# Ending a four-layer graph kernel: one chain of factors for all 26 tiles instead of two, halves in the last row block, a second slot for the last sums

## The chip, the cores and the metric

The kernel runs on one core of one Trainium2 chip. Times are microseconds of device time for one execution. The time before is the median of three runs. The profile is one more execution, taken by the hardware profiler; its span runs from the first to the last instruction of the core, and its own time is a little longer than its span.

## The reference, cut to what matters

Four graph layers follow each other on a node matrix of 3327 x 64 (padded to 26 tiles of 128 nodes) with a dense 0/1 adjacency matrix. Each is a pre-norm residual layer: `h = relu(layernorm(x))`, `x = x + layer(h, adj)`. The change concerns the fourth layer alone, a hyperbolic attention:

```python
left, right = x_t @ w_att[:D, 0], x_t @ w_att[D:, 0]
adj_att = sigmoid(left[:, None] + right[None, :] + b_att[0]) * adj
x_local = logmap(x[:, None, :], x[None, :, :], c)          # for every pair of nodes
support_t = einsum('ij,ijd->id', adj_att, x_local)         # sums over neighbours
return proj(expmap(x, support_t, c), c)                    # pointwise per node
```

The kernel does not form `x_local`. The logarithm of a pair becomes a weight (an arctangent of a Gram product, plus a constant), so that the sums over neighbours are matrix products of the weights with rows of x. What is left after these sums (`expmap`, `proj` and the residual) is pointwise per node: it comes down to two numbers for each node, here called ah and am, and to `X += Xr*ah + M*am`, where Xr holds the layer's scaled input and M the sums.

## The kernel before, in words

The function `hyperbolic_series` serves the first and the fourth layer; the fourth call (`then is None`, with r, `done` and `checks`) is the one that changes. Its nodes i are cut into four chunks of 4, 3, 3 and 3 tiles in each of two halves (`chunks`, line 380): half o holds tiles 0 to 12 or 13 to 25, and one chunk covers columns of both halves at once, so that a work tile is 128 x 2 x 512 or 128 x 2 x 384. For every chunk a loop goes over the 26 row blocks b of the neighbours. That is K = 104 work tiles, listed in `tiles`.

The order on ACT, DVE, PE and POOL in the loop is written out by hand (`tc.manual_schedule`, closed by `region.close()` on line 945). For work tile k:

- `sigmoid(k)` (line 610): ACT makes the sigmoid (L614), POOL multiplies it with the adjacency mask, which is fp8 in this call (L616);
- `products(k)` (line 618): PE makes the Gram product in a PSUM slot (L627, L628), one of four;
- `angle(k)` (line 630): ACT takes the arctangent in place (L633);
- `weights(k)` (line 635): DVE adds a constant and multiplies with the masked sigmoid (L637);
- `sums(k)` (line 640): PE adds the tile to the chunk's sums. L646 uses every tile by itself, one product for each half o; L654 takes the tiles in pairs, after the second one.

After row block 25 of a chunk, the closures in `later` run: `out_of` copies the two parts of the sums from PSUM to SBUF (ACT, L664), `back` turns both parts with six PE transposes into one slot (L673), and `to_m` and `to_m2` form, for that chunk's columns, the inner product hm with Xr (L684, L692), M0 (L685), the norm mm (squares L686 on ACT, sum L693) and M itself (L690).

`factors` (line 701) is a generator of some 55 small DVE operations on one column of numbers per tile, with one tanh on ACT (L780). It holds two inverse roots by bit tricks (`root_by_bits`, L128 to L142), and most of its steps use the result of the step before. Before the change it runs twice: for `early` = the first ten tiles of each half (20 tiles), and for `late_` = the last chunk (6 tiles). The first 16 steps of the early one stand in the loop's iteration j = K/2 (line 919). Then `both` issues late and early steps in turn, and when early has its factors, `moves` for these 20 tiles stands between the remaining late steps: 20 scalings of M on ACT (L877, one tile each), and on DVE four times Xr*ah (L870), four times X+Xr (L882) and four times X+M (L886). `done` stores these tiles (L2073, SP queue). Moves and a store for the late six tiles follow.

At the very end every engine loads a flag from SBUF and branches on it (L2124; a fallback that isn't taken on these data stands behind the branch). SP does this after it has issued the last store.

Of the kernel before, what the change touches and what calls it, by code (L numbers as in the profile page):

```python
# [14 lines left out]
AF = mybir.ActivationFunctionType  # L15
OP = mybir.AluOpType
# [33 lines left out]
def tile_gnn4(ctx: ExitStack, tc: tile.TileContext, x, adjT, att0, b0, w1, bias1, w_gat, a_gat,  # L50
# [8 lines left out]
    def room(**kw):  # L59

        return tc.tile_pool(reuse_waits="tile", **kw)
# [288 lines left out]
    def hyperbolic_series(r, params, ok, masks=None, done=None, ahead=None, then=None, checks=None):  # L350
# [18 lines left out]
        with ExitStack() as st:  # L369
# [232 lines left out]
            def by_tiles(t, c):  # L602

                return (t.rearrange("p (o t) d -> p o t d", o=2) if len(t.shape) == 3 else
                        t.rearrange("p (o t) -> p o t", o=2))[:, :, c[0]:c[0] + c[1]]

            def new(name, c, dtype=F32, rows=P, **kw):
                return wk.tile([rows, 2, W], dtype, name=name, **kw)[:, :, :c[1] * P]

            def sigmoid(k):  # L610

                c, b = tiles[k]
                sig = sigs[k] = new("sig", c, bufs=7)
                A.activation(sig, leftB[c], AF.Sigmoid, bias=right[:, b:b + 1])  # L614
                adj = adjs.pop(k) if masks is None else halves(masks[b // 2][:, b % 2, :], c)
                G.tensor_tensor(sig, adj, sig, op=OP.mult)  # L616

            def products(to):

# [14 lines left out]

            def weights(k):
                slot, sig = Ls.pop(k), sigs[k]
                V.scalar_tensor_tensor(sig, slot[:, :, :tiles[k][0][1] * P], PC, sig, op0=OP.add, op1=OP.mult)  # L637
                slots.append(slot)

            def sums(k):  # L640
# [25 lines left out]
                    slots.append(acc.pop(c))  # L666

            def back(j, c, a):
                slot = slots.pop(0)
                for o in range(2):  # L670
                    for i in range(c[1]):
                        cs = slice(i * P, (i + 1) * P)
                        PE.transpose(slot[:, o, cs], a[:, o, cs], ident)  # L673
                later[j, 1] = lambda: to_m(j, c, slot)

            def to_m(j, c, slot):
                pm = slot[:, 0, :c[1] * P].rearrange("p (t o d) -> p o t d", o=2, d=D)
                if ahead is not None and c == chunks[-1]:
                    prod = ahead.same.rearrange("p o i -> p (o i)").bitcast(F32)[:, :4 * c[1] * D].rearrange(
                        "p (k o t d) -> p k o t d", k=2, o=2, d=D)  # L680
                else:
                    prod = wk.tile([P, 2, 2, 4, D], F32, name="prod", bufs=1)[:, :, :, :c[1], :]
                pm0 = slot[:, 1, :c[1] * P].rearrange("p (t i o d) -> p o t i d", i=2, o=2, d=32)
                V.tensor_mul(prod[:, 0], by_tiles(Xr, c), pm)  # L684
                V.reduce_sum(by_tiles(M0, c), pm0[:, :, :, :, 0], axis=AX.X)  # L685
                A.activation(prod[:, 1], pm, AF.Square)  # L686
                later[j + 1, 0] = lambda: to_m2(j + 1, c, slot, pm, prod)
# [164 lines left out]
                both = value_of(factors(lambda name: tp.tile([P, T], F32, name=name), (0, HT)))  # L852
                return [f.rearrange("p o t -> p (o t)") for f in both]

            def place_in_loop(name):

                return checks.adjs[2][:, len(places) * T:(len(places) + 1) * T]

            found = {}

            def of_tiles(c):
                found[c] = yield from factors(place_in_loop, c)

            def moves(c, pieces):


                ah, am = found[c]

                def scaled(a, f, ts):
                    V.tensor_mul(a, a, f[:, :, :, None].to_broadcast([P, f.shape[1], f.shape[2], D]))  # L870

                cut = [(slice(o, o + n), slice(t, t + m)) for o, n, t, m in pieces]
                for os, ts in cut:
                    for o in range(os.start, os.stop):
                        for t in range(ts.start, ts.stop):
                            m = by_tiles(M, c)[:, o, t, :]
                            A.activation(m, m, AF.Copy, scale=am[:, o, t:t + 1])  # L877
                for os, ts in cut:
                    x, a = by_tiles(X, c)[:, os, ts], by_tiles(Xr, c)[:, os, ts]
                    scaled(a, ah[:, os, ts], ts)  # L880
                    yield
                    V.tensor_add(x, x, a)  # L882
                    yield
                for os, ts in cut:
                    x, m = by_tiles(X, c)[:, os, ts], by_tiles(M, c)[:, os, ts]
                    V.tensor_add(x, x, m)  # L886
                    yield
                done(c)

            def both(one, two):  # L890

                for _ in one:
                    next(two, None)

            early, late_ = (0, 10), chunks[-1]
            moving = of_tiles(early) if done is not None else iter(())

            sigmoid(0)
            for j in range(-1, K // 2 + (5 if then is None else 1)):
                for k in (2 * j - 2, 2 * j - 1):  # L900
                    if 0 <= k < K:
                        sums(k)
                for i in range(2):
                    k = 2 * j + i
                    products(2 * j + 3 + i)
                    if 0 <= k < K:
                        weights(k)
                    if i == 0 and (j, 0) in later:
                        later.pop((j, 0))()
                    products(2 * j + 4)  # L910
                    if k + 2 < K:
                        angle(k + 2)
                    if k + 3 < K:
                        if masks is None and k + 5 < K:
                            load(k + 5)
                        sigmoid(k + 3)
                    if i == 1 and (j, 1) in later:
                        later.pop((j, 1))()
                    if j == K // 2:
                        for _ in range(8):  # L920
                            next(moving, None)
                if at(2 * j + 10, 1):
                    columns(at(2 * j + 10, 1))
                if ahead is not None:
                    ahead.step(j)
                if checks is not None:
                    checks.step(j)
                if then is not None and j == K // 2 - 1:
                    table_of(AF.Exp)

            if then is not None:
                then(SimpleNamespace(Xr=Xr, M=M, slots=slots, later=later, factors=all_factors, close=lp.close,
                                     ahead=ahead, close_all=hs.close))
                return
            def of_early():
                yield from moving
                yield from moves(early, [(o, 1, t, 5) for o in range(2) for t in (0, 5)])

            rest = of_early()
            both(of_tiles(late_), rest)  # L940
            for _ in rest:
                pass
            for _ in moves(late_, [(0, 1, 0, 3), (1, 1, 0, 3)]):
                pass
            region.close()
            lp.close()

    def hyperbolic(att, b_att, r, min_norm, min_norm2):

# [1115 lines left out]
        for ts in HALVES:  # L2065
            nc.sync.dma_start(X[:, ts, :], x.rearrange("p (t d) -> p t d", d=D)[:, ts, :])

    def store():
        nc.sync.dma_start(out.rearrange("p (t d) -> p t d", d=D), X)

    def store_tiles(c):
        ts = slice(c[0], c[0] + c[1])
        nc.sync.dma_start(out.rearrange("p (h t d) -> p h t d", h=2, d=D)[:, :, ts, :], X2[:, :, ts, :])  # L2073

    ok = const.tile([P, 4], F32, name="ok")
    load()
# [9 lines left out]
    with ExitStack() as ms:  # L2086
        mid, rs = [ms.enter_context(ExitStack()) for _ in range(2)]
        masks = [None] * (T // 2)
        degs = []

        def make_masks(ks):
            pool = ms.enter_context(room(name=f"masks{ks[0]}", bufs=1, side="right"))
            for k in ks:
                masks[k] = pool.tile([P, 2, NP], F8, name=f"mask{k}")

        def right():
            make_masks(range(T // 2 - EARLY // 2))
            pool = rs.enter_context(room(name="middle", bufs=1, side="right"))
            degs.append(pool.tile([P, NP // 2], F32, name="deg"))
            return degs[0]  # L2100

        make_masks(range(T // 2 - EARLY // 2, T // 2))
        pool = mid.enter_context(room(name="own", bufs=1))
        own = [pool.tile([P, 2, CW], F32, name=f"own{k}") for k in range(2)]
        hyperbolic_series(None, params, ok[:, 0:1], ahead=Ahead(masks, zo, own),
                          then=lambda e: plain_decay(
                              e, right, masks, zo, wt, bias, gru, of_r[0],
                              lambda *a: plain_gat(masks, zo, degs[0], first, wg, gru, *a)))
        rs.close()
        mid.close()  # L2110
        hyperbolic_series(r3, params3, ok[:, 2:3], masks, store_tiles, checks=Late(zo))
    V.reduce_sum(ok[:, 1:2], zo, axis=AX.X)


# [55 lines left out]
```

## Time and profile before

| what | us |
|---|---|
| median of the three runs | 728.15 (726.80 to 729.39) |
| the profiled execution's own time | 726.02 |
| its span | 724.3 |
| PE busy | 628.6 (87%) |
| DVE busy | 543.4 (75%) |
| ACT busy | 539.4 (74%) |
| POOL busy | 430.3 (59%) |
| last PE work of the loop (start of the last L654 group) | 696.30 |
| DVE's last addition to X starts / the last store is issued | 716.9 / 717.3 |

A group's line in the profile names line, engine and operation, then `out<-in` with the shapes, a count, busy time and the mean of one in ns, then the idle time before it and what ended it. In the timeline the first two columns are start and duration in us from the span's start. POOL's spans are rough, and the ends of matmuls are modelled.

### The profile page before, as it was taken

The page shows a single profiled execution, that of the slowest core. Times are in us where ns is not written, and L with a number is a line of the kernel's source. Part 1 is how long each engine was busy: PE and PEld are TensorE (multiplying, and loading weights), DVE is VectorE, ACT ScalarE, POOL GpSimd, SP SyncE. Part 2 cuts the span into 40 slices and gives each one's busy share as a digit, 9 for nine tenths or more (in the row PEclk, how much of TensorE's full clock was granted, in tenths as well). Part 3 has the DMA queues.
Part 4 walks back from the last instruction along what each step waited for, and adds up shares of the span by engine and source line. Part 5 has one row for each costly group of instructions (what it writes and reads, how often), then busy time and mean ns, then how long its engine had stood idle before and what let it go on. Part 6 is the DMA issues. An engine that isn't in the chain of part 4 may idle for free.

```text
span 724.3 us, 12042 instructions
## 1 busy us (share of the span) xinstructions
PE 628.6 (87%) x4227; PEld 253.2 (35%) x4227; DVE 543.4 (75%) x1055; ACT 539.4 (74%) x705; POOL 430.3 (59%) x326
## 2 busy tenths in 40 slices
PE   0799999989999799989998997169999999999950
PEld 0522233333333243435445642052223333333310
DVE  6867778777777799999746239887667878777776
ACT  2788888888888785687871586258888889888833
POOL 2699999989999301116620000048888787888820
PEclk9999999999999999999999999569999999999985
DMA  3898898888888716489940000203334334444001
GB/s 64 307 296 268 265 277 264 276 274 271 271 251 279 262 44 243 133 289 349 403 183 2 1 1 1 94 19 94 95 95 134 106 116 149 119 119 118 2 4 50
DMA packets 61751, 119.26 MB, mean 165 GB/s; under 512 B 9552, under 2 KB 34032, under 8 KB 61680
## 3 DMA queue, kind: packets, MB, share of 16 engines
q1 hardware_dynamic: 57328, 118.38, 50.7%
q10 hardware_dynamic: 4352, 0.02, 0.3%
q8 instruction: 35, 0.57, 0.3%
q14 instruction: 36, 0.29, 0.1%
HBM read 115.64 MB, written 0.88 MB: 161 GB/s over the span
## 4 chain that ended last, share of the span: by engine, by line
PE 64%; DVE 16%; POOL 5%; issue 4%; DMA 4%; ACT 3%; SPq 2%; ACTq 1%; POOLq 0%; DVEq 0%
PE slot L646 18%; PE slot L654 10%; PE slot L627 9%; PE slot L628 8%; PE slot L1580 6%; PE slot L1879 5%; POOL sig L616 5%; PE slot L1594 4%; DMA adj<-in 3%; DVE same L1475 2%; PE slot L1995 1%; ACT sig L614 1%; DVE mask L1563 1%; DVE sig L637 1%; DVE X L1633 1%
## 5 line engine op out<-in xcount | busy, mean ns | idle before, releaser
L637 DVE SCALAR_TENSOR_TENSOR sig<-slot,sig 128x768 f32<-128x768 f32 (+1 forms) x208 | 212.6, 1022 | 110.6 <-POOL sig L616 109.4
L633 ACT ACTIVATE slot<-slot 128x768 f32<-128x768 f32 (+1 forms) x208 | 177.3, 852 | 56.7 <-PE slot L628 56.5
L616 POOL TENSOR_TENSOR sig<-adj,sig 128x768 f32<-128x768 f32 (+1 forms) x104 | 201.1, 1963 | 14.8 <-ACT sig L614 10.5
L614 ACT ACTIVATE sig<-leftB,right 128x768 f32<-128x768 f32 (+1 forms) x208 | 203.3, 977 | 0.1
L616 POOL TENSOR_TENSOR sig<-mask,sig 128x768 f32<-128x768 fp8e4 (+1 forms) x104 | 173.3, 1679 | 39.9 <-ACT sig L614 39.0
L646 PE MATMUL slot<-sig,Xr 128*64 128x384 f32 (+1 forms) x832 | 169.6, 526 | 7.5 <-DVE sig L637 7.4
L627 PE MATMUL slot<-XC,XT 128*128 128x384 f16 (+1 forms) x416 | 142.2, 342 | 2.7 <-ACT sum L664 1.7
L628 PE MATMUL slot<-XF,XE 73*128 73x384 f16 (+1 forms) x416 | 141.3, 340 | 0.0
L654 PE MATMUL slot<-sig,X 128*32 128x384 f32 (+1 forms) x832 | 94.2, 525 | 0.0
L1586 ACT ACTIVATE w<-slot,ebias 128x832 bf16<-128x832 f32 x76 | 69.2, 952 | 25.1 <-PE slot L1580 24.7
L646 PEld LDWEIGHTS slot<-sig,Xr 128*64 128x64 f32 x832 | 49.6, 135 | 89.1 <-issue 61.0
L627 PEld LDWEIGHTS <-XT 128*128 128x128 f16 x416 | 40.6, 98 | 93.8 <-issue 67.4
L1580 PE MATMUL slot<-mask,rest 128*128 128x416 fp8e4 x208 | 53.9, 341 | 5.2 <-ACT adj L1586 2.8
L1580 PE MATMUL slot<-mask,after 128*128 128x416 fp8e4 x208 | 53.3, 339 | 1.1 <-DVE deg L1604 1.1
L628 PEld LDWEIGHTS <-XE 73*128 73x128 f16 x416 | 40.8, 98 | 28.5 <-issue 4.2
L1475 DVE TENSOR_SCALAR_CACHE_REDUCE same<-late 128x832 fp8e4<-128x832 f32 x48 | 48.4, 1009 | 0.0
L219 POOL TENSOR_TENSOR mask<-mask,offdiag 128x128 fp8e4<-128x128 fp8e4 x26 | 15.8, 617 | 46.7 <-PE slot L1580 46.7
L436 POOL MEMSET X<- 128x832 f32 x2 | 1.6, 792 | 67.8 <-DVE o L2024 67.8
L1879 PE MATMUL slot<-mask,own 128*64 128x416 fp8e4 x416 | 38.8, 340 | 2.2 <-DVE deg L1604 2.2
L654 PEld LDWEIGHTS slot<-sig,X 128*32 128x32 f32 x832 | 16.4, 108 | 67.7 <-issue 66.1
L1594 PE MATMUL slot<-w,h 128*64 128x416 bf16 x304 | 34.0, 345 | 0.0
L542 PE MATMUL pt<-ident_h,Xp 128*64 128x128 f16 x32 | 2.6, 313 | 35.5 <-ACT Xp L481 35.5
(351 smaller groups left out, 686.1 us busy)
## 6 DMA issues: line engine op xcount, KB each, us to landing
adj<-in SPq DMA_DIRECT2D x78, 384.0 KB, 4.6
late<-in SPq DMA_DIRECT2D x48, 416.0 KB, 3.2
adj<-in SPq DMA_DIRECT2D x17, 832.0 KB, 7.2
adj<-in SPq DMA_DIRECT2D x27, 512.0 KB, 5.1
ahead<-in SPq DMA_DIRECT2D x14, 832.0 KB, 8.2
ahead<-in SPq DMA_DIRECT2D x16, 416.0 KB, 5.9
own<-in SPq DMA_DIRECT2D x16, 416.0 KB, 5.7
own<-in SPq DMA_DIRECT2D x8, 832.0 KB, 6.6
```

Source lines behind the costliest of these rows:

```text
L614: A.activation(sig, leftB[c], AF.Sigmoid, bias=right[:, b:b + 1])
L616: G.tensor_tensor(sig, adj, sig, op=OP.mult)
L627: PE.matmul(L[:, o, :c[1] * P], XT[:, rows], XC[c][:, o, :], start=True, stop=False)
L628: PE.matmul(L[:, o, :c[1] * P], XE[:KE, rows], XF[c][:, o, :], start=False, stop=True)
L633: A.activation(L, L, AF.Arctan, scale=PA / SX ** 2)
L637: V.scalar_tensor_tensor(sig, slot[:, :, :tiles[k][0][1] * P], PC, sig, op0=OP.add, op1=OP.mult)
L646: PE.matmul(acc[c][o * D:(o + 1) * D, 0, :n], Xr[:, b, :], sigs[k][:, o, :], start=b == 0, stop=b == T - 1)
L654: PE.matmul(acc[c][q:q + 32, 1, :n], X0[:, b - 1 + i, :], w[:, o, :], start=b == 1, stop=b == T - 1, tile_position=(0, q))
L1580: PE.matmul(cnt[o][:, h, :BK], w, cols(k, o, h), start=w is after and steps[k][1] == T - 1, stop=True, skip_group_check=True)
L1586: A.activation(ws[k][:, o, :, :], cnt[o][:, :, :BK], AF.Exp, scale=-LN2, bias=ebias)
L1594: PE.matmul(acc[c][o * D:(o + 1) * D, h, :BK], parts[i][:, b, :], w[:, o, h, :], start=b == T - 1 and i == 0, stop=b == 0 and i == 1)
L1879: PE.matmul(acc[k][o * D:(o + 1) * D, :], w, mask[:, o * HP + k * BK:o * HP + (k + 1) * BK], start=n == 0 and i == 0, stop=n == T - 1 and ...
```

## The change

In the fourth layer only:

- Row block 25 of the last chunk (k = 103) goes through POOL (L616) and DVE (L637) as two halves of 128 x 384 instead of one 128 x 768 operation. PE's L646 products of the two halves o wait for their own half.
- Each of the last chunk's two turned parts gets a slot of its own; `to_m` reads the first part from one and the second from the other.
- `factors` runs once for all 26 tiles, after the loop. It stands outside the hand-written order, so that its place in the queues is the scheduler's. The in-loop early steps, `of_tiles`, `moves`, `both` and `place_in_loop` go away; the factors' tiles come from a pool that is opened after the loop's is closed.
- The moves are made on halves of 13 tiles (832 elements a partition): Xr*ah twice, X+Xr twice. M*am is done by ACT for tiles 0 to 21 and by one DVE operation for tiles 22 to 25. Then three additions X+M follow, of 13, 7 and 6 tiles, each with a store of its own: three stores of contiguous tiles with 128 rows instead of two stores of two pieces per partition.

```diff
+            def parts_of(k):
+                return (slice(0, 1), slice(1, 2)) if k == K - 1 and then is None else (slice(0, 2),)
...
-                G.tensor_tensor(sig, adj, sig, op=OP.mult)
+                for os in parts_of(k):
+                    G.tensor_tensor(sig[:, os], adj[:, os], sig[:, os], op=OP.mult)
...
-                V.scalar_tensor_tensor(sig, slot[:, :, :tiles[k][0][1] * P], PC, sig, op0=OP.add, op1=OP.mult)
+                for os in parts_of(k):
+                    V.scalar_tensor_tensor(sig[:, os], slot[:, os, :tiles[k][0][1] * P], PC, sig[:, os],
+                                           op0=OP.add, op1=OP.mult)
...
-                slot = slots.pop(0)
+                to = [slots.pop(0)]
+                to.append(slots.pop(0) if j > K // 2 and then is None else to[0])
...
-                        PE.transpose(slot[:, o, cs], a[:, o, cs], ident)
+                        PE.transpose(to[o][:, o, cs], a[:, o, cs], ident)
...
-                pm0 = slot[:, 1, :c[1] * P].rearrange("p (t i o d) -> p o t i d", i=2, o=2, d=32)
+                pm0 = to[1][:, 1, :c[1] * P].rearrange("p (t i o d) -> p o t i d", i=2, o=2, d=32)
...
-                    if j == K // 2:
-                        for _ in range(8):
-                            next(moving, None)
...
-            rest = of_early()
-            both(of_tiles(late_), rest)
-            for _ in rest:
-                pass
-            for _ in moves(late_, [(0, 1, 0, 3), (1, 1, 0, 3)]):
-                pass
             region.close()
             lp.close()
+            with room(name="hse", bufs=1) as tp:
+                ah, am = all_factors(tp)
...
+                own = slice(T - 4, T)
+                for t in range(own.start):
+                    A.activation(M[:, t, :], M[:, t, :], AF.Copy, scale=am[:, t:t + 1])
+                for ts in HALVES:
+                    scaled(Xr, ah, ts)
+                    added(Xr, ts)
+                scaled(M, am, own)
+                for ts in HALVES[0], slice(T // 2, T - 6), slice(T - 6, T):
+                    added(M, ts)
+                    done(ts)
...
-        nc.sync.dma_start(out.rearrange("p (h t d) -> p h t d", h=2, d=D)[:, :, ts, :], X2[:, :, ts, :])
+    def store(ts=slice(0, T)):
+        nc.sync.dma_start(out.rearrange("p (t d) -> p t d", d=D)[:, ts, :], X[:, ts, :])
```

`scaled(a, f, ts)` multiplies `a[:, ts, :]` in place by the factor of each tile, and `added(a, ts)` adds `a[:, ts, :]` to X in place.

More of the change, by code (lines that the diff above doesn't have):

```diff
@@ L672, in back, with to_m @@
                         cs = slice(i * P, (i + 1) * P)
-                        PE.transpose(slot[:, o, cs], a[:, o, cs], ident)
-                later[j, 1] = lambda: to_m(j, c, slot)
-            def to_m(j, c, slot):
+                        PE.transpose(to[o][:, o, cs], a[:, o, cs], ident)
+                later[j, 1] = lambda: to_m(j, c, to)
+            def to_m(j, c, to):
+                slot = to[0]
                 pm = slot[:, 0, :c[1] * P].rearrange("p (t o d) -> p o t d", o=2, d=D)
@@ L853, in all_factors @@
                 return [f.rearrange("p o t -> p (o t)") for f in both]
[L855 to L896, printed above, removed]
             sigmoid(0)
@@ L934, in hyperbolic_series, with scaled, added @@
                 return
-            def of_early():
-                yield from moving
-                yield from moves(early, [(o, 1, t, 5) for o in range(2) for t in (0, 5)])
-            rest = of_early()
-            both(of_tiles(late_), rest)
-            for _ in rest:
-                pass
-            for _ in moves(late_, [(0, 1, 0, 3), (1, 1, 0, 3)]):
-                pass
             region.close()
             lp.close()
+            with room(name="hse", bufs=1) as tp:
+                ah, am = all_factors(tp)
+                def scaled(a, f, ts):
+                    V.tensor_mul(a[:, ts, :], a[:, ts, :], wide(f[:, ts]))
+                def added(a, ts):
+                    V.tensor_add(X[:, ts, :], X[:, ts, :], a[:, ts, :])
+                own = slice(T - 4, T)
[8 more added lines that the diff above has]
+                    done(ts)
     def hyperbolic(att, b_att, r, min_norm, min_norm2):
@@ L2066, in load @@
             nc.sync.dma_start(X[:, ts, :], x.rearrange("p (t d) -> p t d", d=D)[:, ts, :])
[L2068 to L2072, printed above, removed]
-        nc.sync.dma_start(out.rearrange("p (h t d) -> p h t d", h=2, d=D)[:, :, ts, :], X2[:, :, ts, :])
+    def store(ts=slice(0, T)):
+        nc.sync.dma_start(out.rearrange("p (t d) -> p t d", d=D)[:, ts, :], X[:, ts, :])
     ok = const.tile([P, 4], F32, name="ok")
@@ L2110, in tile_gnn4 @@
         mid.close()
-        hyperbolic_series(r3, params3, ok[:, 2:3], masks, store_tiles, checks=Late(zo))
+        hyperbolic_series(r3, params3, ok[:, 2:3], masks, store, checks=Late(zo))
     V.reduce_sum(ok[:, 1:2], zo, axis=AX.X)
```

## The prediction

> **What bounds the kernel now.** I read the page first (PE is busy 87% of the span), then the timeline of the last 35 us, where the whole change lies. The loop bodies of the fourth layer stay as they are, so PE's bound there stays too. From row block 103 on, one thing waits for the next:
>
> ```profile
> 692.90 1.56 POOL L616 TENSOR_TENSOR sig<-mask,sig 128x768 f32<-128x768 fp8e4 x1 [0.53 <-ACT sig L614]
> 694.50 0.96 DVE L637 SCALAR_TENSOR_TENSOR sig<-slot,sig 128x768 f32<-128x768 f32 x1 [1.14 <-POOL sig L616]
> 695.51 0.87 PE L646 MATMUL slot<-sig,Xr 128*64 128x384 f32 x4 [0.68 <-DVE sig L637]
> 696.30 0.85 PE L654 MATMUL slot<-sig,X 128*32 128x384 f32 x8
> 697.22 0.87 ACT L664 ACTIVATE sum<-slot 128x384 f32<-128x384 f32 x2 [3.70 <-PE slot L654]
> 697.77 0.93 PE L673 MATMUL slot<-ident,sum 128*128 128x128 f32 x6 [0.61 <-ACT sum L664]
> 698.74 0.56 DVE L684 TENSOR_TENSOR prod<-Xr,slot 128x384 f32<-128x384 f32 x1 [0.57 <-PE slot L673]
> 699.46 0.49 ACT L686 ACTIVATE prod<-slot 128x384 f32<-128x384 f32 x1 [1.37 <-DVE M L685]
> 699.99 0.55 DVE L693 TENSOR_REDUCE mm<-prod 128x6 f32<-128x384 f32 x1
> 700.46 0.15 DVE L716 TENSOR_TENSOR late<-M,kb 128x6 f32<-128x6 f32 x1
> ```
>
> No engine is full here; it is a relay. At 700.46 the late factors start. The windows show what follows: DVE is busy without a gap until the last addition ends, then 7 us run without any compute.
>
> ```profile
> 700.46:708.72 8.26, 0.00 (x0) 0.00 (x0) 8.09 (x84) 0.43 (x2) 0.00 (x0) 0.50 0.02 6
> 708.72:717.25 8.53, 0.00 (x0) 0.00 (x0) 8.36 (x34) 6.42 (x26) 0.00 (x0) 0.50 0.14 56
> 717.25:724.30 7.05, 0.00 (x0) 0.00 (x0) 0.00 (x0) 0.00 (x0) 0.00 (x0) 0.50 0.18 61
> ```
>
> Columns: stretch, us, then busy time and count of PE, weight loads, DVE, ACT, POOL. So the late factors take from 700.46 to 715.23 (14.8 us for 6 tiles), since steps and moves of the early tiles stand between them.
>
> The price of a step is in DVE's timeline of the early chain, where it runs alone:
>
> ```profile
> 697.12 0.18 DVE L130 TENSOR_TENSOR late<-late 128x20 f32<-128x20 f32 x1
> 697.34 0.18 DVE L132 TENSOR_TENSOR late<-late 128x20 f32<-128x20 f32 x1
> 697.55 0.18 DVE L134 SCALAR_TENSOR_TENSOR late<-late 128x20 f32<-128x20 f32 x1
> ...
> 715.18 0.36 DVE L870 TENSOR_TENSOR Xr<-Xr,late 128x192 f32<-128x192 f32 x1
> 715.58 0.36 DVE L882 TENSOR_TENSOR X<-X,Xr 128x192 f32<-128x192 f32 x1
> 715.85 0.35 DVE L870 TENSOR_TENSOR Xr<-Xr,late 128x192 f32<-128x192 f32 x1
> 716.24 0.36 DVE L882 TENSOR_TENSOR X<-X,Xr 128x192 f32<-128x192 f32 x1
> 716.51 0.74 DVE L886 TENSOR_TENSOR X<-X,M 128x192 f32<-128x192 f32 x2
> ```
>
> Start to start is 0.21: 0.18 of duration and 0.035 until a dependent step starts. An independent one starts about 0.08 before its forerunner's end (695.37, then 695.46), so 0.10 apart. A 6-wide step takes 0.16, so width costs about 1 ns an element.
>
> [...] the trace's 128x832 multiplication (L480) takes 1024; for 320 [...] L882 takes 491. [...] the square (L686) starts after DVE's L685, which reads the same slot, though it needs nothing of it. [...] L877 takes 332, and 20 of them 4.88 us, 0.244 apart. [...]
>
> **The parts.**
>
> *Halves of block 103.* POOL's two shapes take 1564 ns for 768 and 2025 for 1024 elements (means of L616 by shape): 1.80 ns an element and 0.18 fixed, so a half is 0.87. DVE's L637 takes 0.955 and 1.226: a half is 0.55. POOL ends its halves at 693.77 and 694.64, DVE's second half runs from 694.68 to 695.23 instead of ending at 695.46. PE then has only the second half's products left (the first half's lie beside DVE's second): L646 begins at 695.28, and L654 follows after 0.79-0.36=0.43, at 695.71 instead of 696.30. **Gain 0.6.** Bounds: if a POOL half cost 1.0, DVE would end at 695.5 and PE alone would give 0.35; if it cost exactly half, 0.78, the gain is 0.75.
>
> *Two slots.* DVE's product L684 needs three of the six transposes, 0.46 earlier (0.93/2). M0 (L685) waits for the other three, at about the time L684 ends, so it stalls little. The square waits for L684 alone, no longer for L685: 0.56 earlier (0.46 and 0.10). It releases mm (L693), and mm the chain. **Gain 0.55** (0.4 to 0.6). The second slot is free by then, and nothing is queued behind.
>
> *One chain.* From its queue order I walk the 26-wide chain with 0.182 a step, 0.218 for a dependent one, 0.24 with a pointer operand (as L775 shows), 0.3 for the reciprocal:
> - the first ten operations, up to the third product: 0.99;
> - eleven dependent steps through the first root: 10 x 0.218 + 0.28 = 2.46;
> - to ACT's tanh and back: 0.48, as at 700.99 to 701.44, then 0.21;
> - 24 mixed steps, most independent of their neighbour: 2.53;
> - ten dependent steps through the second root: 2.18, and 0.22 for the last two.
>
> That is 9.07 from the first step to the first move. The early chain's steps in the loop were hidden beside PE's last sums; now all tiles start after them, but the width is nearly free. Bounds: 0.21 to 0.23 a dependent step moves this by 0.25 either way.
>
> *Moves.* DVE: four operations of 832 at 0.94 apart, 3.74; the 256-wide scaling of M, 0.34; three additions of 832, 448 and 384. ACT's 22 scalings start with am: the 13th is done 3.3 after it (earlier than DVE needs it, at 4.1), the 20th 5.0 after. So the second addition waits some 0.1 for ACT. The last one ends 6.2 after the chain. ACT is next in line here: at 0.33 apart it would be late.
>
> So chain and moves take 9.07+6.23=15.3, where 700.46 to 717.25 is 16.8 now. **Gain 1.5** (1.1 to 1.9). In-place X, the pool opened later and the removed in-loop steps I cost at nothing: the queue order shows no new wait of the first steps on another engine, and the in-loop steps stood where DVE waits for PE.
>
> *Stores.* A store is now 128 rows; the trace's 128x832 loads on SP are issued in 0.33, where the last store of 256 pieces takes 0.575. SP loads the flag after it. **Gain 0.24.** The additions end 0.55 or more apart, so three issues at 0.38 don't queue. SP then branches and is away for 2.9 us, before it looks at the stores' semaphores:
>
> ```profile
> SPq L2124 <- SPq L2124: 2.9, 1, 2.9
> ```
>
> Under this the data are hidden: they start 1.3 after the first issue (714.75 to 716.05 now); 852 KB at the 353 GB/s of today's first store (655 KB in packets from 716.05 to 717.91) take 2.4, landing 0.6 (the second's last packet ends at 719.44, its semaphore is up at 720.04). That is 4.3 after the first issue; SP looks at 1.1 (the third issue) + 4.35 = 5.5.
>
> **Sum:** 0.6+0.55+1.5+0.24 = 2.9. Against the profiled execution's own 726.0 us (span 724.3) this gives 723.1, 0.40% less. The median of the runs, 728.15, stands 2.1 above that execution; I take the same 2.9 from it: **725.2 us**.
>
> **Rivals.** *ACT sets the end:* if its scalings go 0.33 apart because they no longer overlap beside 832-wide DVE work, the 22nd is done 7.3 after am, the last addition ends 1.7 later than I have it, and 1.2 is left: 727.0. Against it: 20 of them went at 0.244 beside DVE. *Halves and slots don't show:* if PE's clock sags or the scheduler's waits hold the transposes together, 0.6 and 0.55 are lost: 726.4. Against it: the program's waits are finer already. *More than I count:* the mixed steps pack tighter and POOL's halves are 0.78: 724.1. *Slower, by the stores:* nearly all 852 KB leave in the last 1.1 us, where before 655 KB had left 2.6 us earlier. If 128 rows drain slowly, landing outlasts SP's 2.9 us. From 239 GB/s down (852 KB in 5.5-1.3-0.6=3.6) it costs; at 131 the gain is gone; at 90 (9.5 us, 5.9 over the cover) it is 731.1. Today's second store, of 768 B pieces, moved 197 KB in 0.88, 223 GB/s, so some cost is possible, but 90 needs less than half of that.
>
> **How the numbers follow.** My forecast has 0.58 (its own range 724.4 to 725.9), ACT as bound 0.18, halves and slots without effect 0.14, more than counted 0.05, slower by the stores 0.05. The measurement tells apart about 0.3%, 2.2 us. Faster: 0.58+0.05=0.63; same: 0.32; slower: 0.05. From 723.6 to 727.2 only the stores' case and the edges of the two end cases are left out.
>
> **What would show it.** In the new profile: two POOL halves of some 0.87 and L646 in two pieces; the square right after L684; first step to first move about 9.1; DVE idle only before the second X+M, on ACT, by 0.1; SP's flag load 0.4 after the third issue, its semaphore waits over at once. A dependent step over 0.23, scalings over 0.25 apart, or SP waiting on a store would make the prediction wrong.

## The result, and the profile after

| | before | after |
|---|---|---|
| median of 22 runs each | 727.41 (724.87 to 732.33) | 725.18 (723.07 to 731.31) |
| ratio, 95% interval | | 0.9968 (0.9951 to 0.9984) |
| the profiled execution's own time | 726.02 | 726.38 |
| its span | 724.3 | 724.6 |

The change saves 2.3 us (727.41 x 0.0032; interval 1.2 to 3.6). The forecast was 725.2, from a gain of 2.9 and the median of three runs, 728.15. With 22 runs the median before is 727.41, so that part of the agreement is luck of the base: the gain itself was put 0.6 too high against the point estimate, within the interval.

**The two spans must not be compared.** They say 0.3 slower. One line of each timeline, the first sigmoid of the fourth layer, shows why. Before:

```profile
485.40 1.15 ACT L614 ACTIVATE sig<-leftB,right 128x1024 f32<-128x1024 f32 x1
```

and after:

```profile
488.97 1.15 ACT L618 ACTIVATE sig<-leftB,right 128x1024 f32<-128x1024 f32 x1
```

The layer starts 3.6 later, behind stages whose instructions and order on each engine are the same in both kernels. In the eleven profiles of this study this start lies between 484.39 and 489.15, with no clear relation to what was edited (e9 returns to this). So I cut the profile at a fixed event, the start of POOL's L621 (L616 before) on block 103, and compare only the tail behind it, which holds the whole change: even the 16 early steps of the loop were executed after it (from 695.37 in the profile before). From the layer's first sigmoid to that event it is 207.50 before, and 207.16 and 207.49 in the two profiles of the changed kernel, so the loop itself did not get longer.

The halves and the slots, in the timeline of the changed kernel:

```profile
696.13 1.71 POOL L621 TENSOR_TENSOR sig<-mask,sig 128x384 f32<-128x384 fp8e4 x2 [0.54 <-ACT sig L618]
697.04 0.56 DVE L643 SCALAR_TENSOR_TENSOR sig<-slot,sig 128x384 f32<-128x384 f32 x1 [0.46 <-POOL sig L621]
697.87 0.56 DVE L643 SCALAR_TENSOR_TENSOR sig<-slot,sig 128x384 f32<-128x384 f32 x1 [0.27 <-POOL sig L621]
698.48 0.19 PEld L653 LDWEIGHTS slot<-sig,Xr 128*64 128x64 f32 x2 [0.45 <-DVE sig L643]
699.27 0.85 PE L661 MATMUL slot<-sig,X 128*32 128x384 f32 x8
700.19 0.87 ACT L671 ACTIVATE sum<-slot 128x384 f32<-128x384 f32 x2 [3.44 <-PE slot L661]
700.74 0.93 PE L681 MATMUL slot<-ident,sum 128*128 128x128 f32 x6 [0.61 <-ACT sum L671]
701.32 0.55 DVE L693 TENSOR_TENSOR prod<-Xr,slot 128x384 f32<-128x384 f32 x1 [2.89 <-PE slot L681]
701.79 0.16 DVE L694 TENSOR_REDUCE M<-slot 128x6 f32<-128x12 f32 x1
701.91 0.49 ACT L695 ACTIVATE prod<-slot 128x384 f32<-128x384 f32 x1 [0.84 <-DVE prod L693]
702.43 0.55 DVE L702 TENSOR_REDUCE mm<-prod 128x6 f32<-128x384 f32 x1
702.90 0.18 DVE L725 TENSOR_TENSOR ca<-M,kb 128x26 f32<-128x26 f32 x1
```

The square (L695) now starts 0.04 after the product's end (701.32+0.55), and no longer behind M0 (L694). DVE's second half of block 103 ends at 698.43, but L661 begins only at 699.27. The windows of the rest (stretch, us, then busy time and count of PE, weight loads, DVE, ACT, POOL):

```profile
702.90:711.89 8.99, 0.00 (x0) 0.00 (x0) 7.94 (x59) 0.22 (x1) 0.00 (x0) 0.50 0.02 5
711.89:718.00 6.11, 0.00 (x0) 0.00 (x0) 6.11 (x9) 5.36 (x22) 0.00 (x0) 0.50 0.02 8
718.00:724.60 6.60, 0.00 (x0) 0.00 (x0) 0.00 (x0) 0.00 (x0) 0.00 (x0) 0.50 0.35 129
```

From the first factor step that needs the last sums, DVE starts 66 operations where it started 115 (the counts in the windows, here and in the prediction, are up to two higher each, as they take in operations that only reach into a window). It is less busy in the chain (7.94 of 8.99, where it was 8.09 of 8.26): with one chain, a step waits for its forerunner and nothing fills the gap. Three steps of the chain, each needing the one before it, start 0.22 to 0.23 apart:

```profile
705.01 0.19 DVE L132 TENSOR_TENSOR nq<-nq,t 128x26 f32<-128x26 f32 x1
705.24 0.18 DVE L134 SCALAR_TENSOR_TENSOR nr<-nq 128x26 f32<-128x26 f32 x1
705.46 0.19 DVE L136 SCALAR_TENSOR_TENSOR ns<-nr,ns 128x26 f32<-128x26 f32 x1
```

SP behind it, from the timeline and the waits:

```profile
717.06 1.43 SPq L2041 DMA_DIRECT2D out<-X  x3
```

```profile
SPq L2092 <- SPq L2092: 2.8, 1, 2.8
```

Three issues in 1.43 (their packets run on to 721.02), and the branch costs SP 2.8, where it cost 2.9 before; it waits for no store.

**The tail by stretches**, before and in every kernel that was run. P is POOL's start on block 103, S ACT's first copy of the sums, F the first factor step that needs them, mv the first move, X the end of the last addition. "By tail" is what the time ratio would be if the tail alone had changed.

| kernel | P to S | S to F | F to mv | mv to X | X to end | P to end | ratio by tail | ratio timed |
|---|---|---|---|---|---|---|---|---|
| before | 4.32 | 3.23 | 8.26 | 8.53 | 7.03 | 31.38 | | |
| after | 4.06 | 2.71 | 8.99 | 6.11 | 6.57 | 28.44 | 0.9960 | 0.9968 (0.9951 to 0.9984) |
| e1, block whole | 4.32 | 2.71 | 8.97 | 6.11 | 6.45 | 28.56 | 0.9961 | 0.9954 (0.9940 to 0.9969) |
| e2, one slot | 4.06 | 2.57 | 9.41 | 6.10 | 6.42 | 28.56 | 0.9961 | 0.9975 (0.9962 to 0.9988) |
| e3, old end | 4.06 | 2.71 | 8.26 | 8.53 | 7.64 | 31.20 | 0.9998 | 1.0003 (0.9993 to 1.0014) |
| e4, column halves | 3.72 | 2.71 | 8.99 | 6.11 | 6.34 | 27.86 | 0.9952 | 0.9953 (0.9937 to 0.9970) |
| e5, moves last | 4.33 | 3.23 | 10.69 | 7.27 | 7.80 | 33.32 | 1.0027 | 1.0029 (1.0014 to 1.0043) |
| e6, old moves | 4.06 | 2.71 | 8.99 | 6.80 | 6.83 | 29.40 | 0.9973 | 0.9971 (0.9956 to 0.9986) |
| e7, one store | 4.06 | 2.71 | 8.99 | 6.11 | 7.07 | 28.93 | 0.9966 | 0.9978 (0.9962 to 0.9993) |
| e8, columns and POOL | 3.72 | 2.71 | 8.98 | 7.35 | 5.78 | 28.55 | 0.9961 | 0.9961 (0.9946 to 0.9975) |
| e9, changed kernel again | 4.06 | 2.71 | 8.98 | 6.10 | 6.50 | 28.36 | 0.9958 | 0.9953 (0.9932 to 0.9973) |

Stretches that an edit leaves alone repeat within 0.02 from profile to profile, so that parts of 0.3 us are read from them. The times can't do that: their intervals reach about 1 us to each side. The last stretch is the loose one: it differs by 0.23 among kernels with the same end (e1, e2, e4, e9, after).

### The profile page after: what moved, and what is told of

It is laid out like the page before. It is cut to its first block, busy times and chain, and to the rows that moved or that the text cites. A ratio compares the mean times of both kernels' runs of the same rounds, so it can differ in the third digit from the quotient of the medians.

```text
span 724.6 us, 11975 instructions
## 1 busy us (share of the span) xinstructions
PE 634.0 (88%) x4227; PEld 258.4 (36%) x4227; DVE 538.8 (74%) x991; ACT 538.2 (74%) x700; POOL 430.0 (59%) x327
## 4 chain that ended last, share of the span: by engine, by line
PE 61%; DVE 16%; POOL 7%; issue 6%; DMA 4%; ACT 3%; ACTq 1%; POOLq 0%; DVEq 0%
PE slot L653 16%; PE slot L661 9%; PE slot L632 8%; PE slot L633 7%; PE slot L1552 6%; POOL sig L621 6%; PE slot L1851 5%; DMA adj<-in 4%; PE slot L1566 4%; DVE same L1447 2%; PE slot L1967 1%; DVE mask L1535 1%; DVE sig L643 1%; ACT sig L618 1%; DVE X L1605 1%
## 5 line engine op out<-in xcount | busy, mean ns | idle before, releaser
L643 DVE SCALAR_TENSOR_TENSOR sig<-slot,sig 128x768 f32<-128x768 f32 (+2 forms) x209 | 212.8, 1018 | 108.9 <-POOL sig L621 108.9
L621 POOL TENSOR_TENSOR sig<-adj,sig 128x768 f32<-128x768 f32 (+1 forms) x104 | 201.1, 1964 | 15.4 <-ACT sig L618 10.9
L621 POOL TENSOR_TENSOR sig<-mask,sig 128x768 f32<-128x768 fp8e4 (+2 forms) x105 | 173.4, 1665 | 41.0 <-ACT sig L618 40.1
L661 PE MATMUL slot<-sig,X 128*32 128x384 f32 (+1 forms) x832 | 94.2, 525 | 0.0
L661 PEld LDWEIGHTS slot<-sig,X 128*32 128x32 f32 x832 | 16.4, 108 | 67.7 <-issue 66.1
```

Source lines behind the costliest of these rows:

```text
L621: G.tensor_tensor(sig[:, os], adj[:, os], sig[:, os], op=OP.mult)
L643: V.scalar_tensor_tensor(sig[:, os], slot[:, os, :tiles[k][0][1] * P], PC, sig[:, os], op0=OP.add, op1=OP.mult)
L661: PE.matmul(acc[c][q:q + 32, 1, :n], X0[:, b - 1 + i, :], w[:, o, :], start=b == 1, stop=b == T - 1, tile_position=(0, q))
```

## The experiments

**e1, block 103 whole again.** Edit of the changed kernel:

```diff
-                return (slice(0, 1), slice(1, 2)) if k == K - 1 and then is None else (slice(0, 2),)
+                return (slice(0, 2),)
```

> The changed kernel with its last row block whole again. Stretch looked at: from POOL's start on row block 103 to ACT's first copy of the sums, 4.32 us before and 4.06 after. Theory (PE runs a block's two products, one for each half o, side by side in different columns of the array, so that splitting them by o leaves the last one its full 0.79): 4.3 again, so the halves gave 0.26 and the whole tail is 0.26 longer than the changed kernel's. Rival, the prediction's own (0.6 from the halves, partly given back elsewhere in the tail): undoing them costs 0.6 of the tail.

P to S is 4.32, as before the change, against 4.06. The halves are worth 0.26 and no more. The timeline of e1 shows both products of the block as one group, and L661 behind it:

```profile
697.81 0.87 PE L653 MATMUL slot<-sig,Xr 128*64 128x384 f32 x4 [0.68 <-DVE sig L643]
698.60 0.85 PE L661 MATMUL slot<-sig,X 128*32 128x384 f32 x8
```

It is 0.79 from start to start for both halves o. In the changed kernel the second half o alone takes 0.79 too (698.48 to 699.27). Where in the array each product lies, the traces do not say.

**e2, one slot for both turned parts.**

```diff
-                to.append(slots.pop(0) if j > K // 2 and then is None else to[0])
+                to.append(to[0])
```

> The changed kernel with both turned parts in one slot again. Stretch looked at: from ACT's copy of the sums to the first step of the factors, 3.24 us before and 2.71 after. Theory (the product waits for six transposes instead of three, and the square waits for the M0 sum as a second reader of the slot): 3.24 again, 0.53 lost, all of it handed on to the end. Rival (most of it comes from the first step of the 26-wide chain being placed better): under 0.2 lost.

S to mv is 11.98 where the changed kernel has 11.70: the slot is worth 0.28 here, half of what was expected. DVE's timeline in e2 says where the rest is:

```profile
698.74 0.55 DVE L701 TENSOR_REDUCE hm<-prod 128x6 f32<-128x384 f32 x1
699.21 0.17 DVE L725 TENSOR_TENSOR ca<-M,kb 128x26 f32<-128x26 f32 x1
699.33 0.18 DVE L727 SCALAR_TENSOR_TENSOR u<-hm,bx 128x26 f32<-128x26 f32 x1
699.43 0.55 DVE L702 TENSOR_REDUCE mm<-prod 128x6 f32<-128x384 f32 x1
```

While DVE waits for the square, two factor steps that need only M0 and hm go ahead of mm (L702). In the changed kernel they come after it. The factors are outside the hand-written order, so the scheduler fills the gap.

**e3, halves and slots alone, with the old chains and moves.** Edit of the kernel before: `parts_of`, its use in `sigmoid` and `weights`, and the two slots of `back` and `to_m`, as the change has them.

> The kernel before with the halves and the second slot alone; factors, moves and stores stay as they were, in two sets. Theory (parts add up): the first two stretches as in the changed kernel, 4.06 and 2.71, then 16.8 from the first late step to the end of the last addition and 7.0 to the end of the span, so 0.8 us faster than the kernel before, 2.1 slower than the changed one. Rival (the early steps in the loop are no longer covered when PE ends sooner, and fall on the path): the 16.8 grows by up to the 0.8 that was won.

Both stretches are shorter by what they are in the changed kernel (0.26 and 0.52), and what follows is untouched; the window from the first late step to the end of the last addition:

```profile
702.47:719.26 16.79, 0.00 (x0) 0.00 (x0) 16.46 (x116) 6.85 (x28) 0.00 (x0) 0.60 0.09 31
```

That is 16.79, as before. Yet the tail is only 0.18 shorter: X to end grew from 7.03 to 7.64. There DVE comes last: it reaches its closing drain at 725.71, SP its own at 725.06. DVE had been back from its branch at 723.28, before SP (723.90); 2.4 us lie between that and its drain, where the kernel before and the changed one have 0.1. Two 8 KB packets of instruction fetch start in this gap (723.91 and 724.46); that DVE waited for them is not shown. The time, 1.0003, shows no gain, and its interval leaves out the 0.9989 that 0.78 us would make. With the old end, the 0.78 won ahead of it is not seen in the time.

**e4, halves by columns.** Block 103 is cut by columns of both o at once, so that PE has half the columns left and not one of two halves o:

```diff
-                return (slice(0, 1), slice(1, 2)) if k == K - 1 and then is None else (slice(0, 2),)
+                h = tiles[k][0][1] * P // 2
+                return (slice(0, h), slice(h, 2 * h)) if k == K - 1 and then is None else (slice(0, 2 * h),)
...
-                    G.tensor_tensor(sig[:, os], adj[:, os], sig[:, os], op=OP.mult)
+                    G.tensor_tensor(sig[:, :, os], adj[:, :, os], sig[:, :, os], op=OP.mult)
...
+                for cs in cols:
+                    for o in range(2):
+                        PE.matmul(acc[c][o * D:(o + 1) * D, 0, cs], Xr[:, b, :], sigs[k][:, o, cs],
```

`weights` and the pair products L662 are cut in the same way.

> The changed kernel with row block 103 halved by columns, 192 of each half o, on POOL, DVE and PE (the pair products of blocks 102 and 103 by column halves too). Theory (a product's time goes with its columns, and the products of one block run side by side): PE has only half a product and half a pair product left after DVE's last half, 0.4 + 0.4, so the stretch from POOL's start to ACT's copy is 3.55 us instead of 4.06. Rival (each group of products costs its 0.8 whatever its width, a fixed latency): 4.1 or more, up to 5.1.

```profile
697.51 0.53 PE L662 MATMUL slot<-sig,X 128*32 128x192 f32 x8
697.98 0.55 PE L655 MATMUL slot<-sig,Xr 128*64 128x192 f32 x4
698.45 0.53 PE L662 MATMUL slot<-sig,X 128*32 128x192 f32 x8
699.05 0.87 ACT L676 ACTIVATE sum<-slot 128x384 f32<-128x384 f32 x2 [3.10 <-PE slot L662]
```

In PE's timeline both o's products of 192 columns take 0.47 (697.98 to 698.45), and the pair products of the first half (697.51) lie ahead of them. P to S is 3.72: 0.60 less than before, the gain that the prediction had given to the other cut. It is 0.17 above the 3.55 expected here: PE begins the last products 0.36 after DVE's last half (697.62), behind the pair products of the first half. The tail, 27.86, is the shortest of all kernels here, 0.58 below the changed kernel's; the times (0.9953 against 0.9968 and, in e9, 0.9953) don't tell the two apart.

**e5, the kernel before with the early moves behind all factors.** This removes the moves from between the late steps:

```diff
-                yield from moves(early, [(o, 1, t, 5) for o in range(2) for t in (0, 5)])
...
             for _ in rest:
                 pass
+            for _ in moves(early, [(o, 1, t, 5) for o in range(2) for t in (0, 5)]):
+                pass
```

> The kernel before, with the moves of the early 20 tiles after both sets of factors instead of between the late set's steps. Stretch looked at: from the first late step to the end of the last addition, 16.79 us before, 15.10 after. Theory (a step that uses the step before it leaves DVE half empty, and the kernel before fills these gaps with the other set's steps and with moves; the single set wins because it has 54 small steps fewer and fewer, longer moves, not because the late steps were held up): late factors end at about 11.0 after their first step, then 7.0 of moves, 17.9 in all, 1.1 slower than before. Rival (the moves held up the late factors, and these set the end): 16.8 or less.

```profile
701.74:712.43 10.69, 0.00 (x0) 0.00 (x0) 10.18 (x99) 2.83 (x12) 0.00 (x0) 0.50 0.02 5
712.43:719.70 7.27, 0.00 (x0) 0.00 (x0) 7.06 (x20) 3.91 (x17) 0.00 (x0) 0.50 0.07 28
```

The windows add up to 17.96 from first late step to last addition, 1.2 more than before. The late factors are done sooner, some 10.7 after their first step instead of 14.8, but the end comes later. The moves had filled the gaps of the dependent late steps (in the early chain of the profile before, a dependent step starts 0.21 after its forerunner, an independent one 0.10): it was not they that held the end up.

**e6, the changed kernel with the old moves and stores** (pieces of five tiles and of three, two stores, ACT for all of M):

```diff
-                for ts in HALVES:
-                    scaled(Xr, ah, ts)
-                    added(Xr, ts)
...
+                moves((0, 10), [(o, 1, t, 5) for o in range(2) for t in (0, 5)])
+                moves(chunks[-1], [(0, 1, 0, 3), (1, 1, 0, 3)])
```

> The changed kernel, one set of factors, but moves and stores in the old pieces: twelve DVE operations of 320 and six of 192 elements, all 26 scalings of M on ACT, two stores of 256 pieces. Stretches looked at: first move to the end of the last addition, 6.11 us in the changed kernel, and from there to the end, 7.03 before and 6.57 after. Theory (ten more operations at 0.07 to 0.08 of fixed cost each, and ACT's last six scalings late): 6.7 to 6.9, and 0.3 more behind it for the longer store issue, so 0.9 of the 2.9 us belong to moves and stores. Rival (the gain lies in the factors alone): 6.2 and 6.6.

```profile
698.65:707.64 8.99, 0.00 (x0) 0.00 (x0) 7.94 (x60) 0.22 (x1) 0.00 (x0) 0.64 0.02 5
707.64:714.44 6.80, 0.00 (x0) 0.00 (x0) 6.62 (x19) 6.31 (x26) 0.00 (x0) 0.50 0.00 1
714.44:721.27 6.83, 0.00 (x0) 0.00 (x0) 0.00 (x0) 0.00 (x0) 0.00 (x0) 0.50 0.37 131
```

The chain stays at 8.99. The new pieces are worth 0.69 (6.80 to 6.11; in e6, DVE waits 0.18 of it for ACT's last scalings), and the end with three stores 0.26 (6.83 to 6.57, about the looseness of that stretch). The fixed cost of 0.07 to 0.08 in the expectation is an estimate from the profile before: 1024 ns for 832 elements (L480) and 491 for 320 (L882) put 158 at a width of zero, and an operation starts about 80 before its forerunner's end. From F to X, e6 has 15.79 and the kernel before 16.79: the single chain is worth 1.0 by itself.

**e7, the changed kernel with one store after the last addition.**

```diff
                     added(M, ts)
-                    done(ts)
+                done(slice(0, T))
```

> The changed kernel with one store of all 26 tiles after the last addition instead of three. Stretch looked at: from the end of the last addition to the end of the span, 6.57 us in the changed kernel. Theory (SP is away for 2.6 to 2.9 us behind its branch, and a store that drains at 350 GB/s lands in this time, 1.3+2.4+0.6 = 4.3 after its issue, when SP looks): 6.4 to 6.8. Rival (128 long rows drain at the 223 GB/s of the last store before, 1.3+3.8+0.6 = 5.7): 1.2 to 1.6 longer, and then the three stores of the change have a hidden share in its gain.

```profile
715.81 0.34 SPq L2041 DMA_DIRECT2D out<-X  x1
```

```profile
SPq L2092 <- SPq L2092: 3.8, 1, 3.8
```

X to end is 7.07, 0.5 more than with three stores; neither expectation had it. The store is issued at 715.81, its packets run from 716.65 to 719.77 (852 KB, 273 GB/s), and its semaphore is up at 720.52. SP branches at 716.79 and goes on at 720.59, after 3.8 instead of 2.8. That looks like a wait for the landing, but it is none: what SP does first there is to check a semaphore that had been up since 667.8, and it comes to the store's own only at 720.77, 0.25 after the landing. The longer absence is SP's own. In each of the eleven profiles, an 8 KB packet of instruction fetch ends 1.1 to 1.3 before SP goes on. It starts 0.9 to 1.4 after SP's branch, but in e7 2.2 after it (718.98), amid the store's packets. That the fetch stood behind these packets is my guess, and not shown. In the changed kernel the last store's semaphore is up at 721.58 and SP is back at 722.34, so that 0.76 is left over.

**e8, column halves, and POOL takes the moves of five tiles.** e4, with POOL doing both products and both additions for tiles 21 to 25, DVE scaling M of tiles 18 to 20, ACT that of 0 to 17, and stores of 5, 13 and 8 tiles:

```diff
+                own = slice(T - 5, T)
+                for ts, f, t in ((own, ah, Xr), (own, am, M)):
+                    G.tensor_tensor(t[:, ts, :], t[:, ts, :], wide(f[:, ts]), op=OP.mult)
+                    G.tensor_tensor(X[:, ts, :], X[:, ts, :], t[:, ts, :], op=OP.add)
+                done(own)
+                own = slice(T - 8, T - 5)
```

> A version meant to beat both: the changed kernel with the last row block halved by columns, and with five tiles (21 to 25) moved wholly by POOL, which is idle there; ACT scales M for tiles 0 to 17, DVE for 18 to 20; three stores. Theory (parts are what their rows say): POOL's start to ACT's copy 3.72 as with the column halves alone; first move to the end of the last addition 5.3 instead of 6.11, bound by ACT's 18 scalings and a 512-wide addition; POOL's four operations of 320 take 0.9 each and end first. So 1.1 to 1.2 us faster than the changed kernel, 4.0 faster than before (ratio 0.9945). Rival (POOL and DVE hold each other up on SBUF when both read two tensors): DVE's 832-wide operations grow beyond 1.1, and the gain in the moves is gone.

The groups of e8 by shape, for its moves (busy us and mean ns behind the bar):

```profile
L917 POOL TENSOR_TENSOR X<-X,Xr 128x320 f32<-128x320 f32 x1 | 1.6, 1637 | 0.0
L912 DVE TENSOR_TENSOR X<-X,Xr 128x832 f32<-128x832 f32 x1 | 1.5, 1540 | 0.0
L912 DVE TENSOR_TENSOR X<-X,Xr 128x512 f32<-128x512 f32 x1 | 1.3, 1345 | 0.0
L909 DVE TENSOR_TENSOR Xr<-Xr,ah 128x512 f32<-128x512 f32 x1 | 1.2, 1212 | 0.0
...
L912 DVE TENSOR_TENSOR X<-X,M 128x832 f32<-128x832 f32 x1 | 1.0, 1012 | 0.0
L909 DVE TENSOR_TENSOR M<-M,am 128x192 f32<-128x192 f32 x1 | 1.0, 1007 | 0.0
L912 DVE TENSOR_TENSOR X<-X,M 128x512 f32<-128x512 f32 x1 | 0.7, 677 | 0.0
```

A DVE addition of 832 elements takes 1540 ns beside POOL and 1012 after it, one of 512 takes 1345 and 677. mv to X is 7.35 where DVE alone needs 6.11, and what the columns gained is lost: the tail is 28.55, none of the 1.1 to 1.2 us expected. The timeline shows how the two engines lie beside each other:

```profile
710.53 2.15 DVE L909 TENSOR_TENSOR Xr<-Xr,ah 128x832 f32<-128x832 f32 x2
710.63 1.51 POOL L916 TENSOR_TENSOR Xr<-Xr,ah 128x320 f32<-128x320 f32 x1 [13.81 <-issue]
712.10 1.17 POOL L916 TENSOR_TENSOR M<-M,am 128x320 f32<-128x320 f32 x1
712.61 2.81 DVE L912 TENSOR_TENSOR X<-X,Xr 128x832 f32<-128x832 f32 x2
713.23 1.64 POOL L917 TENSOR_TENSOR X<-X,Xr 128x320 f32<-128x320 f32 x1
714.94 1.19 POOL L917 TENSOR_TENSOR X<-X,M 128x320 f32<-128x320 f32 x1
715.34 1.01 DVE L909 TENSOR_TENSOR M<-M,am 128x192 f32<-128x192 f32 x1
```

The ends of the single operations alternate, DVE at 711.55, POOL at 712.14, then 712.68, 713.27, 714.15, 714.86, 715.41, 716.13, and DVE at 716.34. DVE's operation of 832 ends 0.88 after POOL's before it, and those of 512 end 0.55 after; undisturbed, two of 832 start 0.94 apart in the changed kernel. So the engines seem to take turns, and each POOL operation takes 0.58 to 0.72 from DVE's path; the overlap in the records then holds the waiting. What they wait for is not shown here.

**e9, the changed kernel once more**.

> The changed kernel once more, beside the version with column halves and POOL on the same chip. Theory: its tail, from POOL's start on row block 103 to the end of the span, is 28.4 us again, whatever its span is, since the stages before it have the same instructions in the same order as before; ratio to the kernel before 0.996. Rival (the later start of the tail in the first profile, 3.2 us, belongs to the change): the last row block starts late against the kernel before again.

The tail is 28.36 (28.44 the first time), and the ratio 0.9953. The fourth layer starts late again, at 489.15. Two profiles of this kernel thus start about 3.7 later than the one of before, and one could suspect the change of it. The times speak against this: with 3.7 lost ahead of the tail and 2.9 won in it, the ratio would be 1.001, outside both timed intervals. What moves this start between 484 and 489 stays open.

## Why the prediction was right, and where it was not

The mechanism was right in the main, and the tail's 31.38-28.44 = 2.94 is the 2.9 of the sum. That it fits so closely is luck, for the split was not right: the halves brought 0.34 less than predicted, chain and moves 0.19 more, the end 0.22 more.

- **Halves: 0.26, predicted 0.6. The step failed.** It said that "PE then has only the second half's products left", with L654 following "after 0.79-0.36=0.43". PE does have only these left, but they take the whole 0.79. The price 0.36 took half of a group for half of its time. The two products of a block, of 64 columns each, run side by side: in the profile before, the last block's two start 7 ns apart, and the two take 0.79 (695.51 to 696.30), as the second alone does after the change (698.48 to 699.27). What remains is DVE's earlier end: 2.30 after POOL's start (698.43-696.13), where it was 2.56, which is 0.26. Even the lower bound, 0.35, was too high, as it rested on the same price. e4 cuts where PE's time does halve, and gets 0.60.
- **Slots: 0.52, predicted 0.55.** L693 no longer waits for all six transposes, nor the square for M0. The square and M0 read different parts of the slot, so no data joined them; the order that ACT kept was a wait on a DVE semaphore, which ended (699.40) just after M0 (699.37). But this is the slot's worth in the kernel before (e3). In the changed kernel it is worth 0.28 (e2), because the single chain lets the scheduler fill the same gap. The two parts of the change overlap by a quarter of a us, and the prediction added them up as if they were apart.
- **Chain: 8.99, predicted 9.07; moves: 6.11, predicted 6.23.** From F to X the gain is 1.69, predicted 1.5. A dependent step is 0.22, 22 scalings on ACT take 5.36, 0.24 apart. DVE's new widths take 1016 to 1022 ns for 832 elements, 617 for 448, 550 for 384 and 417 for 256; an operation of 832 starts 0.94 after the other, as assumed. The wait for ACT before the second X+M does not show. e6 splits the 1.69: 1.0 is the single chain, 0.69 the larger pieces. The prediction gave as the reason for 14.8 us of late factors that "steps and moves of the early tiles stand between them". They did, but e5 shows that this cost nothing: with the moves behind them, the end comes 1.2 later. What gains is that 39 of the small steps are gone from F to X (49 operations fewer, 10 of them moves), not that late steps are no longer held up.
- **Behind the last addition: 0.46, predicted 0.24.** From the last issue to SP's branch it is 1.39 where it was 1.68. Of these 0.29, only 0.155 is the shorter issue that the prediction priced (0.42 where it was 0.575; it had put 0.33). The rest is SP's load of the flag: 0.85 where it was 0.99, but it varies (0.52 in e7). The remaining 0.17 lies within the looseness of this stretch, so that how much of the 0.46 belongs to the change stays open.
- **The rivals.** ACT did not set the end (0.24 apart, not 0.33). Halves and slots did show (0.26 and 0.52), with a granted PE clock of 1.00 from P to S and 0.98 from S to F. The stores did not outlast SP's absence: 0.76 is left over, though they moved at 274 GB/s (852 KB from 717.91 to 721.02) and not at the 353 assumed. With all 852 KB leaving after the last addition (e7), half a us comes back, but through SP's longer absence: even there the store had landed 0.25 before SP looked at it.

## What to carry to other kernels

Before half a group of matmuls is priced at half its time, see in the trace whether its members run side by side; where they did here, half of the members took the whole 0.79 us (the changed kernel), and half of the columns of the moving operand 0.47 (e4). Gains that fill the same gap don't add (the slot gave 0.52 in e3 and 0.28 in e2): price the second one with the first in place. And where a chain of small dependent steps ends a kernel, the number of operations on it counted here and not their width (a 6-wide step takes 0.16 us, a 26-wide one 0.19): one chain of 26 columns was worth 1.0 us against two of 20 and 6, though work can fill the gaps between its steps (put behind them in e5, it adds 1.2 us). An idle POOL was no help to DVE in e8, where both read two SBUF tensors: DVE's 512-element addition took 1345 ns beside POOL and 677 after it.

## What the hardware showed that was not expected

- One product of 64 columns takes the same 0.79 us as two side by side.
- DVE and POOL on SBUF operands at the same time: a 512-element DVE addition at 1345 ns instead of 677, 320-element POOL operations at 1167 to 1637 (none ran undisturbed), with ends that alternate as if one engine ran at a time.
- The end behind the branch is not fixed by SP alone. With the same last store, the stretch was 0.6 longer in e3, where DVE reached its closing drain 0.65 after SP; in e5 it was 0.92 after.
- One store of 852 KB issued 1 us ahead of SP's branch goes with an absence of 3.8 us behind it, where all other kernels have 2.6 to 2.9.
- The start of the same fourth layer differs by up to 4.8 us between profiles. A span is then no measure for a change of 3 us; a cut at a fixed event is.
